# A four-layer network in one kernel: three engines issue the Toeplitz stretches in program order

## Chip, cores and metric

The kernel runs on one core of a Trainium2 chip. The metric is the time on the device, in microseconds (us), of one execution of the whole kernel. Everything is computed in float32.

## What is computed

The input x has the shape (8, 56, 56, 192): batch, height, width, channels. Four layers follow each other, each with a residual: x = x + layer(GroupNorm(x)). Layers 0 and 1 are gated Toeplitz layers, layer 2 is a ConvNeXt block (a 7x7 depthwise convolution, then an MLP), layer 3 is windowed attention with 7x7 windows and six heads. The part that the change is about, layers 0 and 1, cut short:

```python
# d = 576 = 3 * 192; a1, a2: (2 * 56, d), from a small MLP over positions, with a decay
p = silu(x @ p_w.T + p_b)
q = silu(x @ q_w.T + q_b)
v = silu(x @ v_w.T + v_b)
qv = q * v
o1 = toeplitz(qv, a1)     # along the width: for each channel, a 56 x 56 Toeplitz matrix
o2 = toeplitz(qv, a2)     # along the height
return (p * (o1 + o2)) @ o_w.T + o_b
```

The reference computes the Toeplitz products with FFTs; the kernel multiplies with the matrices themselves.

## The kernel before, in words

**Work units.** A Toeplitz layer is cut into three kinds of work. Each is a Python generator that issues a bit of work and yields what this bit is reckoned to cost TensorE, in microseconds.

- The *projection* `tno_qv` makes qv for two pairs of samples. For 256 tokens at a time it loads x (L222, from SP) and normalises it on ScalarE (L228, six instructions). Then come units: `unit` multiplies 128 tokens with up to 512 columns of the weights (matmuls L245, into one or two PSUM buffers), and VectorE adds the bias out of PSUM (L254). `multiply`, for the unit before, is called just ahead of the next one: silu on ScalarE (L264), q times v on VectorE (L267) into a tile with the tag t4, and a store of that tile to DRAM from SP (L270). The store is not issued at once but one unit later.
- The *Toeplitz* work `tno_toeplitz` takes qv of two pairs of samples, in nine blocks of 64 channels, for each block once along the height and once along the width: 18 starts in a stretch. `load` brings a block of qv: for the first direction in two halves, one from SP and one from ScalarE (L317), for the second from ScalarE (L320). `matrices` loads the Toeplitz matrices in two halves from ScalarE (L331). The loads for start n + 2 are issued at the end of the `along` part of start n. `along` multiplies (matmuls L343: 16 small ones to a channel group, four copies of the result by ScalarE to a piece, L350). `turned` transposes back on TensorE (L360), seven at a time into one PSUM buffer, and VectorE copies them to the sum (L363) or adds them to it (L366). A finished half block goes to DRAM from GpSimd (L376). A start has four pieces: two of `along`, two of `turned`, each of four PSUM buffers.
- The *output* `tno_out` works in steps of 224 tokens. It loads x (L112, two tiles at a time) and the sum o1 + o2 (L436) from SP, normalises x on VectorE (L442, into a t4 tile), and multiplies with the gate's weights for this tile (L460, L475, L488, L496) and, for the tile before, with the output weights (L470, L484, L492, L499). Silu for the gate on ScalarE (L504, four instructions into two t4 tiles, and L521), the gate's products on VectorE (L531, L532), the bias and the residual on VectorE (L514, L517), statistics for the next layer (L537), store from GpSimd (L115).

**The order.** `weave` runs one lane of projection or output work and gives in Toeplitz pieces between its steps, by their reckoned costs. There are six lanes (`tno_layers`): the first projection alone; then four lanes, each with one Toeplitz stretch woven in: a projection; outputs and a projection; outputs and a projection; outputs; and last the outputs of the second half of layer 1, which are woven into the start of the ConvNeXt layer. Near the end of a generator, when 90% of its reckoned time is done, `weave` calls the next generator of the following work until it yields something other than None, so that its first loads are issued early. A generator which yields None asks to be called once more, at the next turn.

This order is the program's. The kernel is built in a tile framework whose scheduler decides, for each engine by itself, in which order the instructions are really issued, from what they depend on and when it reckons that they can run. It also decides which of a pool's buffers a tile gets. All engines, and the DMA queues of SP, ScalarE and GpSimd, follow the order that the scheduler wrote[...].

**Buffers.** The pool for PSUM has four buffers of two banks each (`bank2`), for all kinds of work. The SBUF pool `tp` has three buffers to each tag: t4 (products of the projection, the normalised tile and the gates of the output work), t6 (x), t8 (z of the projection, the sum in the output work).

**Attention.** Layer 3 runs in units of a half of a sample. `order` says, in three groups of four places, whether a place between the attention's own steps is given to the projection for the next unit (0) or to the output of the previous one (1). The output (`out`) has two parts: 128 channels and then 64. Each multiplies (L1271) and adds bias and residual on VectorE (L1282).

Of the kernel before, what the change touches and what calls it, by code (L numbers as in the profile page):

```python
# [15 lines left out]
AX = mybir.AxisListType  # L16
PSUM = bass.MemoryType.PSUM
DRAM = bass.MemoryType.DRAM

B, H, W, C = 8, 56, 56, 192  # L20
T = H * W
# [10 lines left out]
def view(ap, offset, dims):  # L32

    return bass.AP(ap.tensor, ap.offset + offset, [ap.ap[0], *dims])


class Net:
# [371 lines left out]
        for f in late:  # L409
            store(*f)  # L410

    def tno_out(self, L, j0, xs, gn, o, ys, gn_next):

# [1 line left out]
        N = 224  # L417
# [10 lines left out]
        def load_x(j, t):  # L428

            x = p.tile([128, 3, 2 * N], F32, name="t6")  # L430
            self.load_pair(x, xs, j, slice(t * N, (t + 2) * N))
            return x

        def load_s(j, t):
            s = p.tile([128, 9, N], F32, name="t8")
            nc.sync.dma_start(s, o[j, :, :, t * N : (t + 1) * N].rearrange("k p t -> p k t"))  # L436
            return s

        def normalize(j, x):
            xn = p.tile([128, 3, N], F32, name="t4")  # L440
            for k in range(3):
                nc.vector.tensor_scalar(  # L442
                    xn[:, k, :], x[:, k, :], gn[:, j, k, 0:1], gn[:, j, k, 1:2], ALU.mult, ALU.add
                )
            return xn
# [96 lines left out]
        before = None  # L542
        x2 = load_x(*tiles[0])
        s = load_s(*tiles[0])
        yield 0.0
        xn = normalize(j0, x2[:, :, :N])
        done = None
        for n, (j, t) in enumerate(tiles):
            self.norm_part()
# [6 lines left out]
            x = x2[:, :, t % 2 * N : t % 2 * N + N]  # L556
            now = (j, t, x, s, st, xn)
            after = None
            if n + 1 < len(tiles):
# [3 lines left out]
                if t % 2:  # L563
                    x2 = x2_next
                at = (t + 1) % 2 * N
                after = tiles[n + 1][0], x2[:, :, at : at + N]
            xn = step(now, before, after)
# [47 lines left out]
    def tno_layers(self, x0, x1, x2, gn, last):  # L615


        tc, nc = self.tc, self.nc
        LS = ("L0", "L1")
        tables = [  # L620
            [self.dram.tile([D1, 112], F32, name=f"{L}_tab{d}") for d in range(2)] for L in LS
        ]
        qvs = {

            j0: self.dram.tile([D1 // 32, 64 * W, 128], F32, name=f"qv{j0}") for j0 in (0, 2)
        }
        o = [self.dram.tile([B // 2, 9, 128, T], F32, name=f"{L}_sum") for L in LS]
        x = (x0, x1, x2)
        with ExitStack() as ctx, ExitStack() as wqp:
            self.wqp = wqp.enter_context(tc.tile_pool(name="wqp", bufs=1, side="right"))  # L630
            self.tp = ctx.enter_context(tc.tile_pool(name="tp", bufs=3))
            Q = lambda i, j0: self.tno_qv(LS[i], j0, x[i], gn[i], qvs[j0])
            O = lambda i, j0: self.tno_out(LS[i], j0, x[i], gn[i], o[i], x[i + 1], gn[i + 1])
            TZ = lambda i, j0: self.tno_toeplitz(j0, tables[i], qvs[j0], o[i])
            QT, OT, TZT = 25 * 2.25 * 5.3, 28 * 10.7, 8 + 72 * 3.2

            with tc.tile_pool(name="tab", bufs=2) as tab:
                self.input_stats(x0, gn[0], 0, tab)
                self.decay_tables("L0", tab, tables[0])
                first = Q(0, 0)  # L640
                for n in range(20):
                    next(first)
                self.input_stats(x0, gn[0], 2, tab)
                none = tab.tile([112, 512], F32, name="none", bufs=1)
                nc.gpsimd.memset(none, 0.0)
                for qv in qvs.values():
                    to = qv[:, T:].rearrange("n (p k) e -> p n (k e)", p=112)
                    nc.gpsimd.dma_start(to, view(none, 0, [[0, D1 // 32], [1, 512]]))
                self.decay_tables("L1", tab, tables[1])
                lanes = [[(first, QT)], [(Q(0, 2), QT)], [(O(0, 0), OT), (Q(1, 0), QT)]]  # L650
                lanes += [[(O(0, 2), OT), (Q(1, 2), QT)], [(O(1, 0), OT)], [(O(1, 2), OT)]]
                self.weave(lanes[0], after=lanes[1][0][0])
            with tc.tile_pool(name="tz", bufs=1) as self.tz:
                self.tms = []
                for i in range(2):
                    tm = self.tz.tile([120, 32 * H + 8], F32, name=f"tm{i}")
                    nc.gpsimd.memset(tm, 0.0)
                    self.tms.append(tm)
                for n, tz in enumerate((TZ(0, 0), TZ(0, 2), TZ(1, 0), TZ(1, 2))):
                    self.weave(lanes[n + 1], tz, lanes[n + 2][0][0], TZT)  # L660
                    if n == 2:
                        wqp.close()
            self.weave(lanes[5], **last())
# [320 lines left out]
    def attention(self, L, xs, gn3, gnd, ys, vd):  # L984
# [6 lines left out]
        nc, tc, inp = self.nc, self.tc, self.inp  # L991
# [7 lines left out]
        if True:  # L999
# [72 lines left out]
            def normalize(b, ra, rb):  # L1072

                ja, sa = b % 4, b // 4
                gb = gr[ja // 2][:, ja % 2 + 2 * sa]
                for c, n, c2 in ((3, 53, 0), (0, 3, 53)):
                    nc.vector.tensor_scalar(
                        view(xa, c2, [[W, 28], [1, n]]),
                        view(ra, c, [[W, 28], [1, n]]),
                        gn3[:, ja, sa, 0:1],  # L1080
                        gn3[:, ja, sa, 1:2],
                        ALU.mult,
                        ALU.add,
                    )
                    nc.scalar.activation(
                        view(xb, c2, [[W, 16], [1, n]]),
                        view(rb, c, [[W, 16], [1, n]]),
                        AF.Identity,
                        bias=gb[:, 1:2],
                        scale=gb[:, 0:1],  # L1090
                    )
# [229 lines left out]
            late = None  # L1321


            order = ((0, 0, 0, 0), (0, 1, 1, 0), (0, 0, 0, 0))
            for n in range(len(units) + 1):
                if n < len(units):
                    (b, hh), (v, qf, kf) = units[n], now
# [234 lines left out]
```

## Time and profile before

| | us |
|---|---|
| median of three executions | 6437.01 |
| lowest and highest | 6429.92, 6446.78 |
| the profiled execution, its own time | 6428.51 |
| span of the profiled execution, first to last instruction | 6426.7 |
| TensorE (PE) busy | 5783.7 |
| VectorE (DVE) busy | 2860.1 |
| ScalarE (ACT) busy | 2148.7 |
| GpSimd (POOL) busy | 635.6 |

In the profile, PE is the matmuls and PEld the loads of their stationary operand. An engine's name with a q (SPq, ACTq) is the issuing of DMAs by this engine. The mean granted clock of TensorE is 0.943 of full speed. The stretches of time in this execution:

| us from the start | what runs |
|---|---|
| 0 to 475 | statistics of the input, decay tables, the first projection |
| 475 to 1115 | first Toeplitz stretch, in a projection |
| 1115 to 1480 | second Toeplitz stretch, in outputs |
| 1480 to 2130 | the same, in the projection of layer 1 |
| 2130 to 2500, 2500 to 3140 | third Toeplitz stretch, in outputs, then in a projection |
| 3140 to 3815 | fourth Toeplitz stretch, in outputs |
| 3815 to 5330 | last outputs, ConvNeXt |
| 5330 to 6427 | attention |

A line of the timeline has the start, the duration, the engine, the source line, the operation with its output and input tiles, the number of instructions gathered in the line, and in square brackets the idle time of the engine ahead of it, with the instruction that ended it. A line of the waits has the waiting engine and line, the releaser, and the idle time in total, the number of times and the longest.

### The profile page before, as it was taken

The numbers are of one execution on the slowest core, as the hardware profiler recorded it, in microseconds if no ns is written. First come the engines' busy times: TensorE is split into PE (matmuls) and PEld (weight loads), VectorE is DVE, ScalarE is ACT, GpSimd is POOL, SyncE is SP. The second block draws the span as 40 slices with busy tenths as digits, with TensorE's granted clock in tenths as the row PEclk, the third lists the DMA queues.
The fourth block names the chain that finished last, engine by engine and source line by source line (L and its number), as shares of the span: only waits on it lengthen the run. The fifth ranks groups of instructions, "written<-read, shape, count | busy, mean of one in ns | idle before, by whom it ended". The sixth has DMA issues, their size and how long they took to land.

```text
span 6426.7 us, 151998 instructions
## 1 busy us (share of the span) xinstructions
PE 5783.7 (90%) x68832; PEld 4566.2 (71%) x68832; DVE 2860.1 (45%) x4858; ACT 2148.7 (33%) x2736; POOL 635.6 (10%) x829
## 2 busy tenths in 40 slices
PE   5998898899999899898888889998999999898897
PEld 3777787787777778777777778885666444666665
DVE  6554555344555444455434343324212322555555
ACT  2444343232444222344232323224323333333332
POOL 0000000000000000000000010000000100333332
PEclk9998999999999999999988999999999999999998
DMA  7448887777675677675698865664444322443432
GB/s 247 116 145 217 225 253 182 209 201 214 182 200 163 178 214 204 186 213 161 174 228 213 256 198 193 218 237 127 166 152 152 93 61 59 73 87 85 90 82 56
DMA packets 1240518, 1078.47 MB, mean 168 GB/s; under 512 B 452704, under 2 KB 1186912, under 8 KB 1224448
## 3 DMA queue, kind: packets, MB, share of 16 engines
q1 hardware_dynamic: 825768, 620.03, 34.9%
q10 hardware_dynamic: 378648, 247.74, 15.1%
q0 software_dynamic: 35456, 200.98, 9.8%
q8 instruction: 541, 8.86, 0.6%
q14 instruction: 105, 0.86, 0.0%
HBM read 712.50 MB, written 356.12 MB: 166 GB/s over the span
## 4 chain that ended last, share of the span: by engine, by line
PE 70%; DVE 10%; DMA 8%; ACT 5%; issue 3%; ACTq 2%; POOL 1%; SPq 1%; DVEq 0%; POOLq 0%
PE bank L245 16%; PE bank L360 7%; PE bank L881 6%; PE bank L460 5%; PE bank L470 5%; PE bank L343 5%; PE bank L742 5%; PE bank L961 4%; PE bank L1155 2%; PE bank L975 2%; DMA qv<-t 2%; PE bank L475 2%; PE bank L492 2%; ACT ot L350 2%; DVE t L254 2%
## 5 line engine op out<-in xcount | busy, mean ns | idle before, releaser
L245 PE MATMUL bank<-wq,t 64*128 64x256 f32 (+5 forms) x8000 | 1319.9, 372 | 66.9 <-ACT ot L350 49.1
L245 PEld LDWEIGHTS bank<-wq,t 64*128 64x128 f32 (+3 forms) x8000 | 1041.0, 189 | 319.1 <-issue 104.9
L264 ACT ACTIVATE t<-t 128x2048 f32<-128x2048 f32 (+1 forms) x300 | 439.9, 1482 | 960.8 <-DVE t L254 872.4
L254 DVE TENSOR_TENSOR t<-bank,wq 128x1024 f32<-128x1024 f32 (+2 forms) x500 | 540.2, 1113 | 477.1 <-PE bank L245 476.2
L360 PE MATMUL bank<-ident,ot 120*128 120x120 f32 x4032 | 549.0, 300 | 162.7 <-ACT ot L350 64.7
L360 PEld LDWEIGHTS bank<-ident,ot 120*128 120x128 f32 x4032 | 494.6, 160 | 222.7 <-DVE s L363 78.1
L504 ACT ACTIVATE t<-bank,wo 128x448 f32<-128x448 f32 x448 | 247.5, 635 | 1065.3 <-PE bank L475 795.8
L343 PE MATMUL bank<-q,tm 56*64 56x112 f32 x18432 | 522.6, 266 | 70.8 <-issue 32.8
L531 DVE TENSOR_TENSOR t<-t,t 128x896 f32<-128x896 f32 x224 | 241.4, 1090 | 752.9 <-ACT t L504 752.0
L343 PEld LDWEIGHTS bank<-q,tm 56*64 56x64 f32 x18432 | 482.1, 138 | 105.9 <-issue 57.1
L350 ACT COPY ot<-bank 128x896 f32<-128x896 f32 x576 | 481.6, 916 | 158.2 <-PE bank L343 157.4
L460 PE MATMUL bank<-t,wo 128*128 128x224 f32 x1792 | 405.1, 382 | 85.8 <-ACT t L504 46.4
L460 PEld LDWEIGHTS bank<-t,wo 128*128 128x128 f32 x1792 | 358.0, 207 | 106.5 <-ACT t L504 58.2
L267 DVE TENSOR_TENSOR t<-t 128x1024 f32<-128x1024 f32 (+1 forms) x300 | 280.5, 955 | 317.0 <-ACT t L264 253.8
L881 PE MATMUL bank<-z,w 128*128 128x448 f32 (+1 forms) x1344 | 413.2, 555 | 2.0 <-ACT h L890 2.0
L470 PE MATMUL bank<-t,wo 128*128 128x224 f32 x1792 | 367.2, 359 | 7.8 <-DVE t L531 4.9
L470 PEld LDWEIGHTS bank<-t,wo 128*128 128x128 f32 x1792 | 346.1, 194 | 11.9 <-DVE t L531 5.3
L363 DVE COPY s<-bank 128x784 f32<-128x784 f32 x288 | 267.7, 970 | 152.7 <-PE bank L360 122.9
L742 PEld LDWEIGHTS bank<-xt,cm 113*112 113x112 f32 x3072 | 309.2, 178 | 36.1 <-issue 31.7
L881 PEld LDWEIGHTS bank<-z,w 128*128 128x128 f32 (+1 forms) x1344 | 182.2, 189 | 205.5 <-issue 196.8
L376 POOL DMA_DIRECT2D L_sum<-s x288 | 141.0, 496 | 1821.5 <-DVE s L366 1816.0
L742 PE MATMUL bank<-xt,cm 113*112 113x108 f32 (+2 forms) x3072 | 317.4, 263 | 3.5 <-ACT h L890 2.4
(141 smaller groups left out, 6814.8 us busy)
## 6 DMA issues: line engine op xcount, KB each, us to landing
q<-qv ACTq DMA_DIRECT2D x36, 3584.0 KB
L_sum<-s POOLq DMA_DIRECT2D x288, 392.0 KB, 7.2
t<-L_sum SPq DMA_DIRECT2D x112, 1008.0 KB
qv<-t SPq DMA_DIRECT2D x192, 512.0 KB
cm<-in_L_cm SPq DMA_DIRECT2D x96, 896.0 KB
tm<-L_tab ACTq DMA_DIRECT2D x144, 392.0 KB
q<-qv SPq DMA_DIRECT2D x36, 1568.0 KB
q<-qv ACTq DMA_DIRECT2D x36, 1568.0 KB
```

Of the source, the lines that this page charges most:

```text
L245: nc.tensor.matmul(pp[:m, b, 256 * j : 256 * j + k], x[rows, j, 2 if part else b, s : s + m], w[rows, part, c0 + c : c0 + c + k],  start=p ...
L254: nc.vector.tensor_add(z[:m, c : c + k, :], view(pp[:m], 0, [[1, k], [256, 4]]), view(bias[:m], c0 + c, [[1, k], [0, 4]]),)
L264: nc.scalar.activation(z[:m, :n, :], z[:m, :n, :], AF.Silu)
L267: nc.vector.tensor_mul(prod[:m, :k], half[:, :, 0], half[:, :, 1])
L343: nc.tensor.matmul(pt[64 * s : 64 * s + 64, r, j * 112 : (j + 1) * 112], tm[rows, c * H : c * H + 64], q[rows, PR * s : PR * s + PR, 4 * c ...
L350: nc.scalar.copy(view(ot, 4 * g, [[112 * 32, 2], [32, 112], [1, 4]]), view(pt, 0, [[512, 2], [1, 112], [112, 4]]),)
L360: nc.tensor.transpose(pz[:, i, :120], ot[:120, at : at + 128], self.ident[:120, :120])
L363: nc.vector.tensor_copy(to, view(pz, 0, [[128, n], [64, 2], [1, 56]]))
L460: mm(gs[c // 2][:, b, c % 2 * 256 : c % 2 * 256 + N], pw[:, 0, 128 * c : 128 * c + 128], xn[:, b], start=c % 2 == 0, stop=False,)
L470: mm(P[:, b, :N], ow[:, c, 0:128], g[:, 4 * b + c], start=c == 0, stop=False)
L742: nc.tensor.matmul(pc[:, 128 * e + 4 * m0 : 128 * e + 4 * m1], cm[:113, e, k, :], xt[:, m0 - 1 + k : m1 - 1 + k, c + e, :], start=n == 0 a ...
L881: nc.tensor.matmul(phs[c][:, s, :TT], w0[rows, part, at : at + 128], z[rows, Z[2 if part else s], :], start=part == flip, stop=part != flip,)
```

## The change

It has three parts.

1. The pool `tz` is opened together with `tc.manual_schedule` for TensorE, ScalarE and VectorE. Inside this block, which holds lanes two to five with their four Toeplitz stretches, these three engines issue their instructions in the order of the program. ScalarE's DMA issues belong to its instructions. SP and GpSimd are still ordered by the scheduler, and the counts of instructions stay equal.
2. `tno_out` takes a flag `early`. With it, the generator yields None after its first loads, and normalises its first tile (L442, three instructions, one t4 tile) at the next turn, when the work before it is still running. It is off for the last outputs, which run outside the block.
3. In attention, the second part of the output is given the fourth place of the middle group in place of the third; a step of the projection takes the third.

```diff
+ENGINES = {mybir.EngineType.PE, mybir.EngineType.Activation, mybir.EngineType.DVE}
...
-    def tno_out(self, L, j0, xs, gn, o, ys, gn_next):
+    def tno_out(self, L, j0, xs, gn, o, ys, gn_next, early):
...
         s = load_s(*tiles[0])
+        if early:
+            yield None
+            xn = normalize(j0, x2[:, :, :N])
         yield 0.0
-        xn = normalize(j0, x2[:, :, :N])
+        if not early:
+            xn = normalize(j0, x2[:, :, :N])
...
-            O = lambda i, j0: self.tno_out(LS[i], j0, x[i], gn[i], o[i], x[i + 1], gn[i + 1])
+            O = lambda i, j0, early=True: self.tno_out(LS[i], j0, x[i], gn[i], o[i], x[i + 1], gn[i + 1], early)
...
-                lanes += [[(O(0, 2), OT), (Q(1, 2), QT)], [(O(1, 0), OT)], [(O(1, 2), OT)]]
+                lanes += [[(O(0, 2), OT), (Q(1, 2), QT)], [(O(1, 0), OT)], [(O(1, 2, False), OT)]]
                 self.weave(lanes[0], after=lanes[1][0][0])
-            with tc.tile_pool(name="tz", bufs=1) as self.tz:
+            in_order = tc.manual_schedule(engines=ENGINES)
+            with tc.tile_pool(name="tz", bufs=1) as self.tz, in_order:
...
-            order = ((0, 0, 0, 0), (0, 1, 1, 0), (0, 0, 0, 0))
+            order = ((0, 0, 0, 0), (0, 1, 0, 1), (0, 0, 0, 0))
```

## The prediction

> **What bounds the kernel now.** I read the page's busy shares first, then the stretches of time with the granted clock, then the waits of TensorE, and then the timeline at the places where the longest of these waits lie.
>
> ```profile
> PE 5783.7 (90%) x68832; PEld 4566.2 (71%) x68832; DVE 2860.1 (45%) x4858; ACT 2148.7 (33%) x2736; POOL 635.6 (10%) x829
> ```
> ```profile
> 475.00:1115.00 640.00, 558.99 (x7491) 482.64 (x7489) 323.18 (x337) 253.07 (x282) 34.80 (x72) 0.93 0.83 221
> 1115.00:1480.00 365.00, 320.41 (x3516) 279.53 (x3520) 149.54 (x271) 94.76 (x152) 24.58 (x39) 0.92 0.76 210
> ...
> 3140.00:3815.00 675.00, 575.95 (x7692) 514.37 (x7693) 270.14 (x435) 192.75 (x279) 53.33 (x93) 0.90 0.82 217
> ```
>
> TensorE is busy 90% and the others at most 45%: the kernel is as long as TensorE's work and its gaps. The columns of the stretches are length, busy PE, PEld, DVE, ACT, POOL, then granted clock, DMA share and GB/s. From 475 to 3815 us lie the four Toeplitz stretches that the change reorders; TensorE idles there 3340 - 2966 = 374 us. That, and the slow clock which follows a gap, is all that a new order can win. Where it lies, by what ended it (us in total, times, longest):
>
> ```profile
> PE bank L360 <- ACT ot L350: 64.7, 27, 6.3
> PE bank L360 <- DVE s L363: 62.6, 53, 5.0
> PE bank L245 <- ACT ot L350: 49.1, 37, 2.9
> PE bank L1271 <- DVE ra L1282: 47.0, 30, 3.6
> PE bank L460 <- ACT t L504: 46.4, 5, 17.5
> PE bank L460 <- DVE t L442: 32.6, 12, 8.1
> ```
>
> Of the last two rows 45 and 16 us lie in three places, the changes from a projection lane to an output lane (near 1115, 2122, 3143 us). The first:
>
> ```profile
> 1111.54 8.74 ACTq L320 DMA_DIRECT2D q<-qv  x1
> ...
> 1115.38 6.30 PE L460 MATMUL bank<-t,wo 128*128 128x224 f32 x16 [5.44 <-DVE t L442]
> ...
> 1118.93 3.34 SPq L270 DMA_DIRECT2D qv<-t  x2
> ...
> 1142.99 2.21 ACT L504 ACTIVATE t<-bank,wo 128x448 f32<-128x448 f32 x4 [29.14 <-DMA qv<-t]
> ...
> 1144.20 3.35 PE L460 MATMUL bank<-t,wo 128*128 128x224 f32 x8 [17.48 <-ACT t L504]
> ```
>
> The first output matmul waits 5.44 us for its normalised tile. The second step then waits 17.48 us for a silu, which waits for a buffer (tag t4) that is still being stored: the two stores were issued at 1118.93, behind the q loads and the weights. The other two changes show 13.6 and 14.1 us in place of 17.48.
>
> The place where the new order may hurt is a Toeplitz block's load among projection units:
>
> ```profile
> 640.74 12.89 ACTq L331 DMA_DIRECT2D tm<-L_tab  x1
> 641.17 0.69 DVE L254 TENSOR_TENSOR t<-bank,wq 128x512 f32<-128x512 f32 x1 [9.47 <-PE bank L245]
> 645.88 2.36 DVE L254 TENSOR_TENSOR t<-bank,wq 128x1024 f32<-128x1024 f32 x2 [4.02 <-PE bank L245]
> 646.63 6.13 PE L360 MATMUL bank<-ident,ot 120*128 120x120 f32 x56
> ...
> 653.73 2.43 ACT L264 ACTIVATE t<-t 128x512 f32<-128x512 f32 x2 [13.86 <-DVE s L363]
> ```
>
> The silu's input was summed by 641.86, but ScalarE was inside the DMA issue of L331 until 653.6. TensorE did not notice: VectorE went on with the adds of the next unit (645.88), ahead of the multiply that needs the silu.
>
> [...]the clock is full or half[...]. The trace agrees: only 1.0 and 0.5 occur, in multiples of 3.41 us, 733 us at half in all[...].
>
> **The change, part by part.** Instruction counts stay equal. In the built program TensorE's order in the stretches is nearly the same; what moves is the order of ScalarE and VectorE, and the times at which SP and ScalarE issue DMAs.
>
> *Lane changes.* The first tile is normalised some five units before the projection ends, so the 5.4 us goes. The last two stores come directly behind SP's half of the first q load, ahead of L112 and the 1.18 MB of wq, and ScalarE's q loads come three output steps later. So the silu's buffer is free about when step one (11.3 us) ends. Removed: 3 x 5.4 + 17.5 + 13.6 + 14.1 = 61 us, and half of 3 x 17 us at half clock = 25. Left: 2 us each for the store, and 4 us each where the late loads are now issued between output steps: 18. Net -68, between -85 and -40.
>
> *Copies ahead of silus.* Before, the scheduler put a silu (1.9 us), or six normalisations L228 (3.06 us, once after waiting 6.1 us for their load), ahead of the copies L350 that transposes wait for. Waits released by L350 are 64.7 + 49.1 and two smaller rows of 11.7 and 6.8, together 132 us. In program order copies come when their matmuls are done. What stays is one copy (0.9 us) for each of the 72 starts, about 70. Net -60 (-100 to -20).
>
> *Buffers of the transposes.* Before, 76 times a set of seven transposes (0.94 us) alternates with its drain (0.97 us) in one PSUM buffer; these waits, by L363 and L366, are 62.6 + 24.9 = 87.5 us, near 1.1 each. The new program cycles through four buffers, so only the drain's slower pace remains, which with the pairs that stand last I take at 0.4 each: -55 (-75 to -20).
>
> *ScalarE's issue in the way.* This is the price. VectorE's multiply of unit k now always stands ahead of the adds of unit k+1. At each of 14 block starts with L317 in projection stretches (8, 3, 3) the silu of unit k lies behind ScalarE's issues; from L317 to the last L331 they take 8.4 to 16 us, summed over the 14, 150 us. TensorE covers only what it can put in four PSUM buffers: the unit in hand (5.55 us), part of which was there anyway; I take 3 us of cover. Cost 150 - 42 = +108. If the queue is as full but the cover is a whole unit it is +70; with none, +150. The starts with L320 block 2 to 5 us, within the cover: 0.
>
> *Output lanes.* In eight places a step follows a step with no piece between, and the xn, now behind L514 and L517, comes about 2 us late: +16. Block starts there (11 to 25 us of issue) now lie ahead of L504, which holds two PSUM buffers: 18 of them at about 1, and the pieces of four sets, 6 in all: +24. Together +40 (+10 to +60).
>
> *Smaller.* The first block's loads of a stretch are waited for: +10 (0 to +20). The early tile holds one of three t4 buffers for five units: +5 (0 to +15). All four copies before the first L331 issue, where one stood behind it: -5 (0 to -10).
>
> *Attention.* The 47 us of L1271 are waits for the drain L1282 of the first part. A piece later, the matmuls that come next in its stead (the projection L1155) take the buffer which that same drain frees: the 2.8 us wait moves to them, and about 0.3 us in each of the 15 units is saved: -4. Not seen in this trace: all of it gone, -47, or a late residual, +20.
>
> Sum: -68 - 60 - 55 + 108 + 40 + 10 + 5 - 5 - 4 = -29 us. The profiled execution took 6428.5 us (span 6426.7), so 6400 on its account; the median of the runs shown is 8.5 above it, so **6408 us** as a median, 0.45% less.
>
> **Rivals.** *Slower: the multiply stuck behind ScalarE's issue.* For: the 13.86 us wait above and four or five like it in the first stretch; today only the free order of VectorE hides it. Against: each block begins with a unit whose matmuls run on. If the cover is nothing (+42)[...], the sum is +37: about 6474 us. It decides from some 11 us lost at each of the 14 starts instead of 7.7. *No change: given back at the lanes.* The late q loads arrive when the first Toeplitz piece wants them and three gaps of 10 us or so return (+30): about 6438. For: these loads moved some 34 us later. Against: the first piece in an output lane comes several steps later. *A larger gain.* If ScalarE's issues are short because the loads are spread more evenly, so that half of the 108 goes[...]: about 6325. For: the L320 starts block only 2 to 5 us. Against: DMA is 69 to 83% busy in these stretches, and nothing is transferred less. *The reordering does nothing*, since the scheduler had the order already: excluded for ScalarE and VectorE, nearly true for TensorE.
>
> **Chances.** Forecast with its own spread (6385 to 6417): 0.38; larger gain 0.15; no change 0.20; slower 0.27. About 0.3% (19 us) is what a measurement can tell from no change. Faster by over that 0.53, within it 0.20, slower 0.27. The bounds above, taken as independent, make about 80 us to either side; I take 6335 to 6490.
>
> **What would show it.** Right: at the three lane changes L460 waits at most 6 us for L504 and the total of 46.4 falls under 15; the row of L360 waiting for L363 falls under 35; the rows released by L350 fall to about 70 together; L245 waiting for L254 rises from 6 to 60 or more, at the L317 starts. Wrong: long waits by a q load at the first pieces; the stretch 475 to 1115 longer by over 80 us (the slower rival; I expect +35 to +50, with the two middle projection stretches unchanged and the lane changes paying for it); the attention stretch of 1097 us shorter by over 20.

## The result and the profile after

The kernel with the change takes 6768.91 us (median of four runs, 6762.89 to 6787.87), the kernel before beside it 6435.61 us: a ratio of 1.0521, with a 95% interval from 1.0495 to 1.0546. It is 333 us slower. The forecast was 6408 us, with a range from 6335 to 6490. Even the rival on the slow side said only 6474. In that figure 24 us, and in the larger gain's 6325 another 30, are an estimate of the author's for the clock, which no trace had shown.

In the code after, the lines of the Toeplitz layers stand two further down (L228 is L230, L245 L247, L254 L256, L264 L266, L267 L269, L317 L319, L320 L322, L331 L333, L343 L345, L350 L352, L360 L362, L363 L365, L366 L368, L442 L444, L460 L462, L504 L506), and those of attention seven (L1155 is L1162, L1271 L1278, L1282 L1289). In the split kernel e4, lines from L399 on stand one further still.

The page after, with the line of the engines' busy time:

```profile
span 6786.1 us, 152002 instructions
...
PE 5782.6 (85%) x68832; PEld 4572.7 (67%) x68832; DVE 2855.9 (42%) x4858; ACT 2148.2 (32%) x2736; POOL 636.2 (9%) x829
```

No engine works longer than before (TensorE 5782.6 against 5783.7 us). The span is 359 us longer, and all of it is idle time of TensorE. By stretches of time, cut at the same changes of lane (length, busy PE, PEld, DVE, ACT, POOL, granted clock, DMA share, GB/s):

```profile
475.00:1300.00 825.00, 582.12 (x7490) 500.07 (x7489) 316.81 (x335) 256.91 (x286) 34.79 (x72) 0.84 0.66 172
1300.00:1862.00 562.00, 470.26 (x5364) 416.41 (x5363) 221.91 (x399) 146.71 (x229) 37.67 (x60) 0.90 0.75 204
1862.00:2404.00 542.00, 457.33 (x4553) 375.89 (x4554) 263.78 (x272) 198.29 (x216) 19.36 (x40) 0.90 0.55 149
```

The first projection stretch takes 825 us where it took 640. The first output stretch takes 562 where it took 537 (the change to a projection came at 1652 us), and the next projection 542 where it took 470. The remaining three are 22, 59 and 31 us longer: projections lose 316 us together, outputs 78. Attention is 32 us shorter (from its first projection matmul to the end 927 us, before 959). The waits of TensorE (total, times, longest) name what came in:

```profile
PE bank L362 <- DVE t L256: 239.5, 32, 14.3
PE bank L247 <- ACT t L230: 139.4, 30, 17.7
PE bank L362 <- ACT t L506: 116.7, 18, 11.6
...
PE bank L345 <- DMA tm<-L_tab: 46.3, 7, 18.3
PE bank L462 <- DVE t L444: 42.5, 10, 8.9
...
PE bank L362 <- ACT ot L352: 38.8, 25, 2.0
...
PE bank L362 <- DVE s L365: 10.3, 2, 6.0
```

The last two rows are what the change was forecast to remove: the transposes wait 39 us for copies where they waited 65, and 10 us for drains where it was 63. The first three rows are what came in their place. The timeline shows where they come from. A start along the height:

```profile
605.53 0.34 ACTq L319 DMA_DIRECT2D q<-qv  x1
...
605.97 15.90 ACTq L333 DMA_DIRECT2D tm<-L_tab  x2
611.00 1.66 PE L362 MATMUL bank<-ident,ot 120*128 120x120 f32 x14
621.97 1.91 ACT L266 ACTIVATE t<-t 128x2048 f32<-128x2048 f32 x1 [15.50 <-issue]
623.91 1.23 DVE L269 TENSOR_TENSOR t<-t 128x1024 f32<-128x1024 f32 x1 [33.34 <-ACT t L266]
625.05 2.35 DVE L256 TENSOR_TENSOR t<-bank,wq 128x1024 f32<-128x1024 f32 x2
626.33 3.06 PE L362 MATMUL bank<-ident,ot 120*128 120x120 f32 x14 [13.68 <-DVE t L256]
```

ScalarE spends 15.9 us issuing the two matrix loads. The silu L266 stands behind them, VectorE's multiply L269 waits for the silu, the adds L256 of the next unit stand behind the multiply, and their PSUM buffers are not free: TensorE stops for 13.68 us in the middle of a transposed piece. This is the chain of the slow rival, link by link. A start along the width, where the prediction saw no cost:

```profile
1171.46 0.35 ACTq L322 DMA_DIRECT2D q<-qv  x1
...
1171.85 11.03 ACTq L333 DMA_DIRECT2D tm<-L_tab  x2
1182.98 1.91 ACT L266 ACTIVATE t<-t 128x2048 f32<-128x2048 f32 x1 [10.32 <-issue]
1184.79 3.04 ACT L230 ACTIVATE t<-t,gn 128x256 f32<-128x256 f32 x6
...
1185.43 6.73 PE L247 MATMUL bank<-wq,t 128*128 128x256 f32 x16 [12.37 <-ACT t L230]
```

Again 11 us of issue, and behind it the normalisation L230 for which the next group's matmuls wait. The kernel before did the same three issues in this order, at a start along the width:

```profile
740.58 0.31 ACTq L331 DMA_DIRECT2D tm<-L_tab  x1
740.96 1.96 ACTq L320 DMA_DIRECT2D q<-qv  x1
742.96 0.42 ACTq L331 DMA_DIRECT2D tm<-L_tab  x1
```

One matrix load stood ahead of the q load, and all three took under 3 us. The page's answers for these lines (duration in ns: least, median, greatest), before and after:

```profile
L331 ACTq DMA_DIRECT2D tm<-L_tab x144: 312/343/16555, 217.9 to 3740.3; - x144
```
```profile
L333 ACTq DMA_DIRECT2D tm<-L_tab x144: 313/8648/17304, 472.9 to 4131.4; - x144
```

The number of loads and their bytes are equal, and the median issue went from 0.34 to 8.65 us. Added up one by one, ScalarE's 216 issues of these three lines took 599 us before and 1124 us after. The matrix loads alone are 1084 of these 1124 us; some of the expectations below start from 1370 and 1415, which is too much.

### The profile page after: what moved, and what is told of

The parts are those of the page before. It is cut to its first block, busy times and chain, and to the rows that moved or that the text cites. A ratio compares the mean times of both kernels' runs of the same rounds, so it can differ in the third digit from the quotient of the medians.

```text
span 6786.1 us, 152002 instructions
## 1 busy us (share of the span) xinstructions
PE 5782.6 (85%) x68832; PEld 4572.7 (67%) x68832; DVE 2855.9 (42%) x4858; ACT 2148.2 (32%) x2736; POOL 636.2 (9%) x829
## 5 line engine op out<-in xcount | busy, mean ns | idle before, releaser
L247 PE MATMUL bank<-wq,t 64*128 64x256 f32 (+5 forms) x8000 | 1363.5, 378 | 153.6 <-ACT t L230 139.4
L247 PEld LDWEIGHTS bank<-wq,t 64*128 64x128 f32 (+3 forms) x8000 | 1068.0, 193 | 425.0 <-ACT t L230 155.6
L362 PE MATMUL bank<-ident,ot 120*128 120x120 f32 x4032 | 553.2, 303 | 406.2 <-DVE t L256 239.5
L362 PEld LDWEIGHTS bank<-ident,ot 120*128 120x128 f32 x4032 | 506.6, 162 | 457.3 <-DVE t L256 247.9
L266 ACT ACTIVATE t<-t 128x2048 f32<-128x2048 f32 (+1 forms) x300 | 443.1, 1485 | 1117.8 <-DVE t L256 708.1
L269 DVE TENSOR_TENSOR t<-t 128x1024 f32<-128x1024 f32 (+1 forms) x300 | 284.4, 955 | 911.8 <-ACT t L266 903.2
L256 DVE TENSOR_TENSOR t<-bank,wq 128x1024 f32<-128x1024 f32 (+2 forms) x500 | 538.4, 1110 | 234.2 <-PE bank L247 233.9
L352 ACT COPY ot<-bank 128x896 f32<-128x896 f32 x576 | 481.6, 924 | 454.1 <-PE bank L345 424.2
L345 PE MATMUL bank<-q,tm 56*64 56x112 f32 x18432 | 517.6, 265 | 123.0 <-issue 50.8
L506 ACT ACTIVATE t<-bank,wo 128x448 f32<-128x448 f32 x448 | 247.6, 634 | 1151.8 <-PE bank L477 682.0
L345 PEld LDWEIGHTS bank<-q,tm 56*64 56x64 f32 x18432 | 480.0, 137 | 152.5 <-issue 113.5
L462 PE MATMUL bank<-t,wo 128*128 128x224 f32 x1792 | 396.0, 377 | 48.0 <-DVE t L444 42.5
L462 PEld LDWEIGHTS bank<-t,wo 128*128 128x128 f32 x1792 | 354.4, 204 | 64.5 <-issue 39.1
L516 DVE SCALAR_TENSOR_TENSOR t<-bank,wo,t 128x448 f32<-128x448 f32 x112 | 76.4, 682 | 751.4 <-PE bank L501 751.4
L472 PEld LDWEIGHTS bank<-t,wo 128*128 128x128 f32 x1792 | 341.9, 192 | 21.7 <-issue 14.6
L365 DVE COPY s<-bank 128x784 f32<-128x784 f32 x288 | 263.5, 964 | 191.7 <-PE bank L362 146.0
```

What stands on the lines that cost most here:

```text
L247: nc.tensor.matmul(pp[:m, b, 256 * j : 256 * j + k], x[rows, j, 2 if part else b, s : s + m], w[rows, part, c0 + c : c0 + c + k],  start=p ...
L256: nc.vector.tensor_add(z[:m, c : c + k, :], view(pp[:m], 0, [[1, k], [256, 4]]), view(bias[:m], c0 + c, [[1, k], [0, 4]]),)
L266: nc.scalar.activation(z[:m, :n, :], z[:m, :n, :], AF.Silu)
L269: nc.vector.tensor_mul(prod[:m, :k], half[:, :, 0], half[:, :, 1])
L345: nc.tensor.matmul(pt[64 * s : 64 * s + 64, r, j * 112 : (j + 1) * 112], tm[rows, c * H : c * H + 64], q[rows, PR * s : PR * s + PR, 4 * c ...
L352: nc.scalar.copy(view(ot, 4 * g, [[112 * 32, 2], [32, 112], [1, 4]]), view(pt, 0, [[512, 2], [1, 112], [112, 4]]),)
```

## Experiments

Theory A: ScalarE's issues became long because program order puts both matrix loads behind the q load, and everything that stands behind ScalarE waits. Theory B: the early tile is a large part of the loss, by the buffer it holds. Theory C: VectorE's fixed order, with the multiply ahead of the next adds, is the cause by itself. All times below are medians, with the ratio to the kernel before, timed beside them, and its 95% interval. The median of the kernel before went from 6420 to 6436 us between the sets of runs, so a difference between versions of different sets is uncertain by some 15 us more.

**The parts of the change.** The program order alone (lines cut short):

```diff
-early=True: self.tno_out(...)
+early=False: self.tno_out(...)
-            order = ((0, 0, 0, 0), (0, 1, 0, 1), (0, 0, 0, 0))
+            order = ((0, 0, 0, 0), (0, 1, 1, 0), (0, 0, 0, 0))
```

> The kernel after with only its first part: program order for three engines; no early tile, attention as before. Theory A (ScalarE's DMA issues became long, because both matrix loads now stand behind the q load, and silus, normalisations and gates wait behind them): within 20 us of the kernel after, 6750 to 6790. Theory B (the early tile takes a t4 buffer and is a large part of the loss): 6650 or less.

Measured: 6791.42 us (1.0556, 1.0533 to 1.058). Theory B falls: without the other two parts the kernel is 22 us slower still. The complement, both other parts and no program order (`in_order = ExitStack()`):

> The kernel before with the early tile and the attention order, and no program order. All theories hold the program order for the cause: 6400 to 6440. If the early tile or the attention order cost by themselves: over 6460.

Measured: 6408.2 us (0.9964, 0.9954 to 0.9974), 22 us faster than before. And the attention order by itself on the kernel before:

> The kernel before with the attention order alone. By the attention stretch of the runs so far (959 us with the old order, 927 to 933 with the new): 25 to 32 us less, 6400 to 6408, and the early tile then costs some 0 to 10 us. By the prediction: 4 us less, 6422 to 6430.

Measured: 6408.02 us against 6422.7 (0.998, 0.9968 to 0.9991): 15 us less, by the interval 6 to 21. In the profiles the attention stretch is 934 us instead of 959. The run time lies at the edge of the first expectation, and the difference is short of it; what the early tile is worth is within the error.

**Whose order it is.** The kernel after with one engine given back to the scheduler, first ScalarE, then VectorE:

```diff
-ENGINES = {mybir.EngineType.PE, mybir.EngineType.Activation, mybir.EngineType.DVE}
+ENGINES = {mybir.EngineType.PE, mybir.EngineType.DVE}
```

> The kernel after with only TensorE and VectorE in program order; ScalarE is left to the scheduler, which again puts a matrix load ahead of the q load. Theory A (long issues on ScalarE): back near before, 6400 to 6460, and the second matrix load's issue is again short at the width starts. Theory C (VectorE's fixed order, the multiply ahead of the next adds, is the cause by itself): 6550 or more, with L362 still waiting over 150 us for the adds L256.

Measured: 6544.42 us (1.0175, 1.015 to 1.02). The issues are short again at the width starts and add up to some 625 us, near the 599 before; yet 115 us of loss stay. So A's number was missed. C's time was missed by a little and its wait by much: L362 waits 86.5 us for the adds L256, where C asked for over 150. What stands out beside it in this profile are the gates (L362 for L506: 84 us) and the lane changes (L462 for the tile L444: 103 us, up to 32 at once). The 115 us were not taken apart further.

```diff
-ENGINES = {mybir.EngineType.PE, mybir.EngineType.Activation, mybir.EngineType.DVE}
+ENGINES = {mybir.EngineType.PE, mybir.EngineType.Activation}
```

> The kernel after with only TensorE and ScalarE in program order; VectorE is left to the scheduler. Theory A: the issues on ScalarE stay long (some 1370 us in the stretches), so the waits for the normalisation L230 (139 us) and for the gates L506 (117 us) stay, and only part of the 240 us behind the adds L256 comes back: 6550 to 6700. Theory C: back to 6460 or less.

Measured: 6673.24 us (1.0377, 1.0352 to 1.0401), inside A's bounds. The 240 us behind the adds are gone, but the time falls by only 96: the wait for the normalisation grows from 139 to 218 us, which fits a TensorE that gets further and meets the next thing behind the same issue. The waits for the drains are back too, 69.9 and 46.6 us.

```profile
PE bank L247 <- ACT t L230: 218.4, 39, 18.3
PE bank L362 <- DVE s L365: 69.9, 63, 3.6
```

**How long the issues are.** The kernel after, with the order of the issues alone changed:

```diff
+                        matrices(n + 2, (0,))
                         loaded.append(load(n + 2))
-                        matrices(n + 2)
+                        matrices(n + 2, (1,))
```

> The kernel after, with one of the two matrix loads L333 of a start issued ahead of the q load and one behind it, as the scheduler had it before; nothing else moved. Theory A: the issue time of L333 in the stretches falls from 1370 us to about 400 to 500 as before, at the width starts from 11 to 18 us to about 3 us each, and the time falls by 200 us or more, to 6480 to 6570. Theory C: the time stays above 6700.

Measured: 6617.38 us (1.029, 1.0267 to 1.0312), 152 us less than the kernel after from two lines moved. The median issue of L333 is 0.37 us again:

```profile
L333 ACTq DMA_DIRECT2D tm<-L_tab x144: 312/368/17277, 471.4 to 3949.9; - x144
```

At the width starts the three issues take 1.8 to 5.4 us, where it was 11 to 18. But at the height starts they take 12 to 28 us, no less than in the kernel after, and the matrix loads' issues add up to 588 us, not 400 to 500 (all three lines: 827). So A's direction held and its size fell short. One of these starts, where the q load is half of the block in rows of 512 bytes:

```profile
586.05 0.34 ACTq L333 DMA_DIRECT2D tm<-L_tab  x1
...
586.49 5.88 ACTq L319 DMA_DIRECT2D q<-qv  x1
...
592.47 14.63 ACTq L333 DMA_DIRECT2D tm<-L_tab  x1
...
607.20 1.91 ACT L266 ACTIVATE t<-t 128x2048 f32<-128x2048 f32 x1 [20.12 <-issue]
```

So at the height starts the old order of the three issues did not make them short again. The traces show another difference. SP issues the other half of the same q block, at some starts within 1 us of ScalarE's issue and at others later. Two height starts of the kernel before, with the same order on ScalarE's queue, show both cases:

```profile
503.30 1.05 ACTq L317 DMA_DIRECT2D q<-qv  x1
504.38 6.84 ACTq L331 DMA_DIRECT2D tm<-L_tab  x1
...
506.44 0.52 SPq L317 DMA_DIRECT2D q<-qv  x1
```
```profile
568.55 0.33 SPq L317 DMA_DIRECT2D q<-qv  x1
568.61 1.86 ACTq L317 DMA_DIRECT2D q<-qv  x1
...
570.50 12.37 ACTq L331 DMA_DIRECT2D tm<-L_tab  x1
```

In the 8 us from ScalarE's q issue on, its queue moved 3332 rows in the first case and 1921 in the second, and SP's queue 128 and 1467, counted from the trace's DMA packets. The mean time of the three issues at the height starts, without the first of each stretch:

| kernel, order on ScalarE's queue | SP's half within 1 us | SP's half later |
|---|---|---|
| before: matrix load, q, matrix load | 19.3 us (13 starts) | 10.7 us (19) |
| e4: the same | 20.2 us (28) | 13.1 us (4) |
| after: q, two matrix loads | 18.6 us (28) | 16.0 us (4) |

In the new program the two halves meet, within 1 us, at 28 of 32 starts, before at 13. When they met, the order on ScalarE's queue made hardly a difference (18.6 to 20.2 us); when they didn't, it did (10.7 and 13.1 against 16.0). This only sorts the starts of runs made for another question: starts in outputs took longer anyway (before 9 to 24 us, in projections 8 to 17) and are not spread evenly, and no run moved SP's half by itself. (In the first stretch of the kernel before, all of it in a projection, it is 15.2 us for three starts that meet and 9.9 for five that don't.)

The split with VectorE free as well:

> The kernel after with both repairs of the first runs: one matrix load ahead of the q load (152 us back by itself), and VectorE left to the scheduler (96 us by itself). If the two are separate costs, they add: 6769 - 248, about 6520. If they are the same waits, seen twice: 6590 to 6620. If what is left was only these two: 6450 or less.

Measured: 6594.02 us (1.0265, 1.0227 to 1.0303). The two repairs give back 152 and 96 us alone and 175 together: largely the same idle time, seen from two sides. Both matrix loads ahead of the q load:

```diff
-                        loaded.append(load(n + 2))
                         matrices(n + 2)
+                        loaded.append(load(n + 2))
```

> The kernel after with both matrix loads L333 ahead of the q load (on ScalarE still). If a matrix load's issue is long because it must wait for what its own queue holds ahead of it (the q load of 1.6 or 3.6 MB): both L333 are short (under 3 us together) at nearly all starts, the wait moves into the q load's own issue only if that has as many pieces, so the width starts block at most 5 us and the height starts (half a q load of 512-byte rows) 10 to 20 us as in the split: 6560 to 6650. If the length comes from two matrix loads in a row, whatever stands ahead: the width starts stay at 10 us or more and the time above 6700.

Measured: 6505.08 us (1.0127, 1.0108 to 1.0146), better than expected. The width starts take 4 to 7 us with few exceptions, the height starts mostly 12 to 18; the sum is 704 us. The long issue has moved into the q load, whose median at the height starts is 8.4 us against 0.33 in the kernel after. So it isn't the matrix load as such that was slow: at the height starts the long issue was that of the load that came last, here the q load, in the kernel after the matrix loads (15.9 us for two at 605.97). The packets of the kernel after fit this: every issue of these loads that took under 1 us found at most 3315 rows in ScalarE's queue that were not yet moved, its own included (99 issues), and every one of more than 6 us at least 3712 (99 issues). In the kernel before the two groups overlap: at most 3575 rows under 1 us (116 issues), at least 3264 over 6 us (42).

**The issues taken off ScalarE.** All three lines issued by SP, which has nothing to compute, in the kernel after and in the kernel before:

```diff
-nc.scalar.dma_start(to.rearrange("p (c w) -> p c w", w=H), src)
+nc.sync.dma_start(to.rearrange("p (c w) -> p c w", w=H), src)
```

(and the same for the two q loads)

> The kernel after with the Toeplitz blocks' loads that ScalarE issues (half of L319, L322, L333) issued by SP instead. Theory A (nearly all of the loss is ScalarE shut in its own DMA issues, with VectorE and TensorE behind it): the waits of L362 for the adds L256 and of L247 for L230 fall under 40 us each, and the time is 6460 or less. Theory C' (the fixed order itself costs, whoever issues): 6550 or more. Theory D (SP's stores L272 then stand behind the long issues, and products wait for their buffers): VectorE's multiply L269 or ScalarE's gates L506 waiting for the store's DMA by over 150 us, and 6550 or more.

Measured: 6250.72 us (0.9728, 0.9687 to 0.9769). This is 518 us less than the kernel after and faster than the kernel before. The wait of L362 for the adds is 20.9 us, within A's bound; that for L230 is 50.4, over it. Theory D shows as 119 us of waits of the multiply for stores, less than its 150.

> The kernel before with the same loads on SP. Theory A: little changes, since the scheduler had kept ScalarE's issues short and VectorE free of them: 6400 to 6450. Theory D: slower by over 50 us.

Measured: 6300.06 us (0.9802, 0.977 to 0.9834). A expected little change, and it is 130 us less. The length of ScalarE's issues explains only a part of it: a run further below (e13) takes nearly all of it away and gains 15 us. What else moved stays open; e6 has no wait of L460 for the gates L504, where e13 has 46.8 us. With the matrix loads alone on SP:

> The kernel after with only the matrix loads L333 on SP; the q loads (half of L319, L322) stay on ScalarE. If the matrix loads are what shuts ScalarE: its issue time in the stretches falls from 1415 us to under 250 and the time is 6300 or less, as with all loads on SP (6251). If the q loads take the long issue over: 6350 or more.

Measured: 6204.44 us (0.967, 0.9653 to 0.9686), 564 us less than the kernel after and 218 less than the kernel before. ScalarE's issues add up to 54 us; 68 of its 72 q loads take under 0.6 us, on the same queue where behind the matrix loads of e9 the median was 2.5 us for L322 and 8.4 for L319. The other four, 6 to 8.8 us, stand at the beginning of a stretch, directly behind half a q load. With all loads on SP and the stores of the products on GpSimd:

```diff
-lambda: nc.sync.dma_start(
+lambda: nc.gpsimd.dma_start(
                     qv[2 * n0 : 2 * n0 + 2 * k, at : at + m, :].rearrange("n t e -> t n e"),
```

> The kernel after with all block loads on SP, and the products' stores L272 on GpSimd in place of SP. With loads on SP the multiply L269 waits 119 us for the stores' DMA, which stand behind the long issues. If these waits reach TensorE: 10 to 40 us less than 6251. If TensorE covers them, or GpSimd's issues are slower: 6240 to 6300.

Measured: 6192.33 us (0.9649, 0.963 to 0.9667), 58 us less than with all loads on SP and the stores there too, more than expected. The multiply's waits for stores fell from 119 to 10.9 us. It has the lowest median of all versions, but the 12 us to the run with the matrix loads alone lie within the intervals.

**What the order is worth without the long issues.** The matrix loads on SP, in the kernel before, and in the kernel after with program order as its only change:

> The kernel before (order of the scheduler, no early tile, old attention) with only the matrix loads on SP. If program order pays once ScalarE's issues are short, as the gains of the prediction (185 us of waits removed, 52 added) say in part: 6250 to 6330, clearly above 6204. If the order is worth nothing by itself and all the gain of the runs with the loads on SP is the moved loads: 6200 to 6235.

Measured: 6405.82 us (0.9976, 0.9965 to 0.9987). That is above both ranges: with the scheduler's order, taking the matrix loads off ScalarE is worth only some 15 us.

> The kernel after with the matrix loads on SP, but without the early tile and with the old attention: the program order alone. Against the run before it, it shows the worth of the order alone; against 6204 that of the early tile and the attention order together. If these two are worth 22 us as on the kernel before: about 6226.

Measured: 6220.05 us (0.9699, 0.9677 to 0.9722). This is close to the 6226 expected. The two differ by the program order only, and by 186 us in its favour. Their waits for the copies and for the gates, first with the scheduler's order, then with program order:

```profile
PE bank L245 <- ACT ot L350: 97.3, 42, 11.1
...
PE bank L360 <- ACT ot L350: 60.9, 26, 5.4
...
PE bank L343 <- ACT ot L350: 49.8, 7, 14.8
PE bank L460 <- ACT t L504: 46.8, 3, 18.1
```
```profile
PE bank L362 <- ACT ot L352: 36.5, 25, 1.9
...
PE bank L247 <- ACT ot L352: 0.9, 1, 0.9
```

Waits for copies fall from 222 us (with 14.3 of L460) to 38, and the 46.8 us for gates at the lane changes are gone. The other two parts add 16 us (6220 to 6204), as on the kernel before within the error. The 186 us belong to this pair: with all block loads on SP, the kernel after leads the kernel before by 49 us (6251 against 6300), all three parts together.

## Why the prediction was wrong, point by point

**The step that failed** is the one on ScalarE's issue, +108 us. It took the durations of the issues from the kernel before ("from L317 to the last L331 they take 8.4 to 16 us"), put the width starts at nothing ("The starts with L320 block 2 to 5 us, within the cover: 0"), and saw in the matrix load that moves behind the copies only a small gain ("All four copies before the first L331 issue, where one stood behind it: -5"). But the program order moves just that load from ahead of the q load to behind it, and the issues became longer with it. In the projections, those at the 14 height starts went from 150 to 230 us in all, at the 14 width starts from 41 to 172 (in the first stretch from 11.9 to 16.7 us and from 3.6 to 12.9 on the mean of eight). In the waits this is 239.5 us for the adds (1.7 of this kind before) and 139.4 us for the normalisation, which the prediction didn't name as queued behind the issue: 379 us where the sum had +108. By the forecast's own reckoning, with 3 us of cover at each start, the measured durations give 318: 130 us of the error are the width starts, 80 the height starts, and 61 a cover that was smaller. The order on the queue explains the width starts, as the split showed (1.8 to 5.4 us where it was 11 to 18); for the height starts the meeting with SP's half is the likelier reason, and not tested by itself.

The kernel before held the warning. At one width start among projection units the scheduler too had put both matrix loads behind the q load:

```profile
671.64 0.35 ACTq L320 DMA_DIRECT2D q<-qv  x1
672.03 0.42 ACTq L331 DMA_DIRECT2D tm<-L_tab  x1
...
672.55 12.35 ACTq L331 DMA_DIRECT2D tm<-L_tab  x1
```

These are 13.3 us, where the other seven of this stretch took 1.8 to 3.3; "2 to 5 us" passes over it.

That the chain is the cause, and not merely beside it, is shown by the matrix loads on SP: with the same order on three engines it is 564 us less, with the scheduler's order 15.

**The cover** was rated somewhat too high: the issue of 15.9 us at 605.97 cost 13.7 on TensorE, the 14.6 us at 1134.45 cost 7.5. Over all, 402 us of issue at the 28 starts in projections, and 27 us more at the first loads of the first stretch, stand against 379 us of waits: 1 to 2 us of cover a start, by this estimate, where 3 was taken. Over whole versions about half of the issue time reaches the run time (an estimate from 1124 us of issue and 6769 us in all; 704 and 6505; 54 and 6204: 0.53 us for each us on the way down).

**Signs.** The wait for the adds was looked for on the projection's matmuls (L245 for L254, from 6 to 60 us or more). It stayed at 7.1 us there and stands on the transposes, with 239.5. Two signs of being wrong came: the first projection stretch is 185 us longer, over the 80 named, and attention shorter by over 20. Two readings were slightly off and change nothing: the DMA share in the stretches is 67 to 83%, and the block starts in outputs take 9 to 24 us.

**Output lanes**: +40 was forecast, from a late tile and about 1 us of overrun at 18 starts. The waits for L506 are 116.7 + 15.8 = 132 us, by the same long issues, which hold the gates and with them two PSUM buffers; with the matrix loads on SP (e10) TensorE has no wait for L506.

**Lane changes**: the 17.5 us kind of wait for the gates is gone, as forecast. The 25 us for the clock were over-rated: they took 17 us at half clock as lying behind each long gap. By the clock's records of the kernel before, the long gaps (to 1144.2, 2147.3 and 3168.4 us) have half clock for 17.1, 13.7 and 13.7 us, of which only 4.7, 5.1 and 4.5 lie behind the gap; with 6.1, 5.9 and 6.1 us behind the 5.4 us gaps ahead of them that is 32 us, worth 16. What was left was under-rated. The tile of the second step now waits for the stores; the early tile and the gates use the same three t4 buffers:

```profile
1304.16 5.86 SPq L272 DMA_DIRECT2D qv<-t  x2
...
1315.23 1.01 DVE L444 TENSOR_SCALAR t<-t,gn 128x224 f32<-128x224 f32 x3 [9.31 <-DMA qv<-t]
1315.77 5.97 PE L462 MATMUL bank<-t,wo 128*128 128x224 f32 x16 [8.87 <-DVE t L444]
```

And the first matrices, issued some 40 us later, are waited for by 46.3 us in all, where 10 was allowed for, beside the 4 at each lane change.

**Copies and buffers of the transposes**: right, and larger than forecast. The waits released by copies fell from 132 to 51 us (-81; forecast -60), those by the drains L363 and L366 from 87.5 to 11 (-77; -55).

**Attention**: the mechanism that was named is there: the wait has moved to L1162 (39.8 us after, 47.0 on L1271 before). The size was wrong, 4 us against 15 timed and 25 to 32 in the profiles, because the clock was left out. Before, the second part's 96 matmuls ran at half clock after their wait (79.7 of their 88.1 us over 15 units); after, they don't (3.7 of 42.0), though the wait of the projection in their stead is as long (up to 3.4 us). The lines of both parts, with a mean of 539 and 419 ns:

```profile
L1271 PE MATMUL bank<-oj,wfc 32*64 32x224 f32 (+1 forms) x2304 | 157.9, 539 | 52.8 <-DVE ra L1282 47.0 <-ACT oj L1260 4.1 <-issue 1.8
```
```profile
L1278 PE MATMUL bank<-oj,wfc 32*64 32x224 f32 (+1 forms) x2304 | 117.7, 419 | 3.1 <-ACT oj L1267 3.0
```

Why the second part ran at half clock behind waits of at most 3.6 us before (L1271, 30 waits), and after mostly at full clock, with the projection's waits of up to 3.4 us ahead of it (L1162, 14 waits), is left open; no run varied it.

**The sum** of the measured waits: 379 + 132 + 46 + 10 (more at L444) - 46 (gates at lane changes) - 81 - 77 - 32 (attention) = +331, against 359 us in the two profiles and 333 in the medians. TensorE's time at half clock rose from 733 to 1047 us, but its busy time did not (5783.7 and 5782.6), so the clock is no further term of the 359. The gains at the copies and buffers came in full, those at the lane changes in part; three costs (issue, outputs, first matrices) were three to five times their estimates.

## What to carry over

When an order changes, the duration of a DMA issue isn't a constant to be carried over: here the median issue of a matrix load was 0.34 us before, 8.65 after and 0.37 with the old order on its queue (e4), and at the height starts of the kernel before the three issues took 10.7 us on the mean where SP's half of q came later, 19.3 where it came within 1 us. So look at which issue stands ahead of which. Before judging an order, give loads like these matrices (56 x 32 rows of 224 bytes) to an engine with nothing to compute: here the same order was worth -186 us with the matrix loads on SP and +362 us (6791 against 6429) with them on ScalarE. When a cost hangs on a wait in front of an engine in program order, count everything behind it, not only the instruction that comes first: here 139.4 us for the normalisation beside 239.5 for the adds.

## What the hardware showed that was not expected

- The issue of one and the same matrix load (56 x 32 rows of 224 bytes) took 0.31 to 17.3 us on ScalarE. Behind a q load of 3584 KB two of them took over 10 us; with one ahead of it and one behind, all three took 1.8 to 5.4 us (e4). In the kernel after, issues of under 1 us came with at most 3315 unmoved rows in the queue, their own included, and those of over 6 us with at least 3712; in the kernel before the figures are 3575 and 3264.
- The half q load (56 x 56 rows of 512 bytes) took 0.33 us to issue in the kernel after, ahead of the two matrix loads, and 8.4 us in e9, behind them (medians).
- At the height starts of the kernel before, the three issues took 10.7 us on the mean when SP's half of q came later, and 19.3 when it came within 1 us.
- With the matrix loads off their queue (e10), 68 of 72 q loads took under 0.6 us to issue (medians 0.34 us for L319, 0.35 for L322). In the kernel after, the issue of a matrix load takes 8.65 us on the median, and its rows, by the packets, are moved in 3.6 us, first to last.
- Two waits behind one long issue didn't add: freeing VectorE and splitting the loads gave 96 and 152 us alone, 175 together.
